# Layer 1 of a two-layer transformer: six edits to who does what, and a new order of the plan

## The chip, the cores and the metric

One core of a Trainium2 chip runs the whole program in one launch. The metric is the device time of one execution in microseconds; lower is better. The engines are TensorE (PE, matrix products; PEld is its weight loads), VectorE (DVE), ScalarE (ACT), GpSimd (POOL) and SyncE (SP, which here only issues DMAs). Each engine works through its own queue strictly in order and waits on semaphores of the others.

## The reference

4096 tokens (2 sequences of 2048) of width 256 pass two layers in float32. Each layer normalizes the tokens and adds to them an attention result and a feed-forward result:

```python
xn = _layernorm(x, axis=-1)
x = x + _L0_attn_ref(xn, ...) + _L0_ffn_ref(xn, ...)
xn = _layernorm(x, axis=-1)
x = x + _L1_attn_ref(xn, ...) + _L1_ffn_ref(xn, ...)
```

Layer 0 is causal attention with 16 heads and a mixture of eight experts (two per token). The change touches layer 1 only. Its attention is against 32 fixed key patterns instead of other tokens: 16 heads give each token 16 rows of 32 scores, and each row passes a sparsemax:

```python
z_sorted = -jnp.sort(-z, axis=-1)
cum = jnp.cumsum(z_sorted, axis=-1)
k = jnp.arange(1, S + 1, dtype=z.dtype)
support = 1.0 + k * z_sorted > cum
k_sup = jnp.sum(support, axis=-1, keepdims=True)
tau = (take_along_axis(cum, k_sup - 1) - 1.0) / k_sup
return jnp.maximum(z - tau, 0.0)
```

The weighted values are projected with `Wo` and get the output bias `bo`. The feed-forward part has a shared expert for all tokens and eight routed ones of which each token takes its best two.

## The kernel before, in words

Layer 0 (lines 274 to 1305) ends with the experts' results written to `oe`, a table in device memory with two result rows per token (the two experts'). Layer 1 begins at line 1311.

**Set-up (1315 to 1383).** SP loads the shared expert's weights (`fg_sb`, `fu_sb`, `fd_sb`). Weights of the attention are folded: `WK` gives all scores from a token in one product, `vbd` holds the values. `three` splits a float32 bias into three bfloat16 parts, so that one extra bfloat16 product (with `row3`, three rows of ones) adds it inside PSUM: `bqK` for the scores, `bo3` for the output. The scratch of this set-up lies in `xn`.

**A plan (class `Plan`, 49 to 127).** The rest of layer 1 is a list of tasks. `add` gives each its engine (`V`, `A`, `G`, `PE`, `S`), an estimated duration in ns, the tasks it comes after, and the buffers (`hold` on a `ring` of n) that it takes (`new`) or uses (`use`). `write` then emits the tasks one after the other as a small simulation: it finds the task that can start first, looks at the others of the same engine that could start almost as early, and of these takes the one with the lowest rank (`RANKS`, 1389) and then the longest way to the end (`way`). So a lower rank goes first. Product durations are stretched by 1.8 for the first 60 us of the plan. The order that comes out is pinned: it is each engine's program order.

The tasks:

- `prepare(grp)`, eight groups of 512 tokens: `add_results` (1425) loads the two rows per token of `oe`, the first into `xn`, the second into one of four landing buffers inside the `z` buffers, and VectorE adds each to `x_sb` (the residual, on chip): two additions of 128x1024. Then the mean and variance (`stat`), reciprocal roots by Newton steps on tiny 128x4 tiles (`roots`, 13 VectorE instructions), normalizing on ScalarE (`norm`), turning on TensorE (`flip`, `keep_`) into `xT`, and router logits.
- `shared(blk)`: the shared expert, its result added to `x_sb` by VectorE.
- `router()`: after the logits of all groups, the best two experts of each token, counts, slots and gates, on VectorE with a few products.
- `dispatch`: 64 indirect DMAs from GpSimd's queue send rows of `xn` to their slot in `buf1`.
- `routed(j)`, 20 blocks of 512 rows: GpSimd fetches the weights (two indirect DMAs), SP loads the rows, VectorE casts the rows' target numbers to integers (`places`, 1712), TensorE turns and multiplies, ScalarE and VectorE activate, and four indirect DMAs of GpSimd's queue send the result to `oe`.
- `scores` and `sparsemax` (1775, 1793), eight of them, each for 512 tokens (128 x 64 rows of 32 scores, 2048 numbers in each partition). The rows are sorted by a 15-stage network: in each stage VectorE makes two comparisons (max and min) and ScalarE copies what stays. Stages alternate between two buffers (`srt`). Then a running sum (`threshold`), minus one times 1/k (`divide`, one VectorE instruction with `invk`), the largest of it (`largest`), and GpSimd subtracts it (`less`). One ring `r_lane` serializes the sparsemaxes on the two buffers. `z` has three buffers.
- `attend(b, c)`: turns, relu, weighting; the second sequence's wait until the first's `project` is through, since both use `oT`. `project(b, h)`: two float32 products and one bfloat16 product (the bias) into PSUM, and VectorE adds the result to `x_sb`.
- `combine(grp)`: `add_results` again for layer 1's routed results; `store(blk)` writes the output.

Most instructions of the plan are recorded by the one helper at line 138, so the profile names them all L138; they are told apart by their tiles.

## Time and profile before

| what | us |
|---|---|
| three runs | 2168.5, 2185.76, 2180.45 (median 2180.45) |
| profiled execution, its own time | 2170.47 |
| its span, first to last instruction | 2168.7 |
| busy: PE, DVE, ACT, POOL | 1927.2, 1408.9, 912.6, 696.2 |
| mean granted TensorE clock | 0.94 |
| set-up of layer 1 begins | 1603 |
| first group normalized (ScalarE) | 1629.8 |
| last group's roots end (VectorE) | 1677.3 |
| first row sent (GpSimd) | 1706.7 |
| first sort comparison (VectorE) | 1717.0 |
| last maximum of a sparsemax ends (VectorE) | 2119.0 |

Times inside the execution count from its first instruction. "Busy" of an engine is time with an instruction running, waits not counted; where an engine stood idle, the profile names in brackets what ended the wait. The eight maxima of the sparsemaxes (`tau`) start at 1765.6, 1822.1, 1867.5, 1912.5, 1957.2, 2003.0, 2058.7 and 2116.8.

### The profile page before, as it was taken

What the parts mean: (1) busy time and instruction counts of PE and PEld (TensorE: products, weight loads), DVE (VectorE), ACT (ScalarE), POOL (GpSimd) and SP (SyncE); (2) the same over time, 40 slices, a digit from 0 to 9 for tenths busy, and PEclk for the clock granted to TensorE, in tenths of its full rate; (3) what the DMA queues carried; (4) which work ended last, traced back from release to release, by engine and by line L of the source; (5) the groups of instructions that cost most, each with busy time, mean ns of one, the idle gap of its engine ahead of it and who ended that gap; (6) DMA issues with size and microseconds to landing.
All of it is one profiled execution on the core that took longest, in us unless ns stands there. A gap on an engine that the chain in (4) does not pass through costs nothing. (4 is left out here: it accounts for less than half of the span.)

```text
span 2168.7 us, 26456 instructions
## 1 busy us (share of the span) xinstructions
PE 1927.2 (89%) x9497; PEld 1074.1 (50%) x9510; DVE 1408.9 (65%) x2010; ACT 912.6 (42%) x1815; POOL 696.2 (32%) x920
## 2 busy tenths in 40 slices
PE   4689998999999999999998899999977985788886
PEld 2344443444444444444443566666746653566664
DVE  4476788677775678777771222222248797999875
ACT  3044455355566555655667111111114232554442
POOL 4232212343335234231001111111210486365652
PEclk8599899899999999999999899999995998999999
DMA  5433311442324333141100712221032123334427
GB/s 155 126 99 101 109 60 38 123 121 96 94 63 138 102 106 99 58 120 53 37 11 11 249 42 85 91 92 49 25 116 70 44 83 112 92 115 123 128 101 232
DMA packets 151064, 204.45 MB, mean 94 GB/s; under 512 B 16393, under 2 KB 116881, under 8 KB 150930
## 3 DMA queue, kind: packets, MB, share of 16 engines
q1 hardware_dynamic: 131264, 151.55, 23.1%
q0 software_dynamic: 16640, 49.41, 6.6%
q10 hardware_dynamic: 3026, 1.77, 0.3%
q8 instruction: 76, 1.25, 0.2%
q14 instruction: 58, 0.48, 0.1%
HBM read 109.13 MB, written 98.79 MB: 96 GB/s over the span
## 5 line engine op out<-in xcount | busy, mean ns | idle before, releaser
L509 ACT ACTIVATE es<-sc 128x512 f32<-128x512 f32 (+3 forms) x1280 | 599.5, 535 | 457.6 <-PE sc L309 443.7
L470 DVE TENSOR_REDUCE part<-s 128x2 f32<-128x1024 f32 (+3 forms) x640 | 650.1, 1058 | 207.2 <-PE s L309 206.1
L309 PE MATMUL sc<-q,ks 128*128 128x512 f32 (+3 forms) x1280 | 426.4, 419 | 19.9 <-ACT es L509 19.5
L309 PEld LDWEIGHTS sc<-q,ks 128*128 128x128 f32 x1280 | 212.5, 192 | 248.3 <-ACT es L509 173.7
L309 PE MATMUL av<-es,va 128*32 128x512 f32 (+3 forms) x2560 | 300.9, 548 | 3.7 <-POOL es L511 2.1
L309 PE MATMUL s<-ks,q 64*128 64x512 f32 (+3 forms) x1280 | 253.0, 447 | 32.8 <-DVE part L470 10.9
L511 POOL TENSOR_SCALAR_AFFINE_SELECT es<-es 128x256 f32<-128x256 f32 x256 | 103.3, 407 | 555.8 <-ACT es L509 554.8
L138 DVE TENSOR_TENSOR srt<-srt 128x1024 f32<-128x1024 f32 (+3 forms) x224 | 231.7, 1072 | 7.0 <-ACT srt L138 0.2
L309 PEld LDWEIGHTS s<-ks,q 64*128 64x128 f32 x1280 | 111.7, 189 | 199.3 <-DVE part L470 113.3
L1276 POOL DMA_INDIRECT oe<-ys,to x72 | 70.0, 972 | 335.1 <-DVE ys L1275 330.2
L1268 DVE TENSOR_TENSOR hT<-ge,pg 128x384 f32<-128x384 f32 x96 | 53.1, 554 | 185.9 <-PE pg L1265 184.7
L1267 ACT ACTIVATE ge<-pa 128x384 f32<-128x384 f32 x96 | 47.1, 490 | 269.2 <-PE pa L1265 269.1
L138 POOL DMA_INDIRECT oe<-xn,to x80 | 100.3, 1254 | 101.4 <-ACT xn L138 82.8
L138 POOL DMA_INDIRECT buf<-xn,slot x64 | 86.1, 1345 | 118.1 <-DVE rc L138 98.9
L1265 PE MATMUL pa<-inT,wi 128*128 128x384 f32 x336 | 123.3, 486 | 0.0
L1265 PE MATMUL pg<-inT,wi 128*128 128x384 f32 x336 | 122.1, 486 | 0.0
L138 ACT COPY srt<-srt 128x1024 f32<-128x1024 f32 (+2 forms) x80 | 66.7, 834 | 120.9 <-DVE srt L138 120.1
L1272 PE MATMUL py<-wt,hT 128*128 128x256 f32 x504 | 112.2, 379 | 0.0
L309 PEld LDWEIGHTS av<-es,va 128*32 128x32 f32 x2560 | 55.6, 109 | 99.7 <-issue 75.9
L1272 PEld LDWEIGHTS py<-wt,hT 128*128 128x128 f32 x504 | 95.8, 190 | 17.5
L1275 DVE TENSOR_SCALAR ys<-py,gates 128x256 f32<-128x256 f32 x72 | 34.8, 484 | 86.2 <-PE py L1272 86.2
L1265 PEld LDWEIGHTS pg<-inT,wi 128*128 128x128 f32 x336 | 63.3, 190 | 42.7
(262 smaller groups left out, 2349.4 us busy)
## 6 DMA issues: line engine op xcount, KB each, us to landing
q<-qd SPq DMA_DIRECT2D x64, 256.0 KB
xn<-oe SPq DMA_DIRECT2D x24, 512.0 KB
buf<-zero SPq DMA_DIRECT2D x20, 516.0 KB
buf<-zero SPq DMA_DIRECT2D x20, 514.0 KB
xn<-buf SPq DMA_DIRECT2D x20, 514.0 KB
rows<-buf SPq DMA_DIRECT2D x8, 1161.0 KB
qd<-hi SPq DMA_DIRECT2D x16, 512.0 KB
qd<-lo SPq DMA_DIRECT2D x16, 512.0 KB
```

The source lines that it names most:

```text
L138: return lambda *a, **k: self.tc.keep_in_program_order(f(*a, **k))
L309: pin(PE.matmul(*args, **kw))
L470: pin(V.tensor_reduce(parts[j][:, i, 2 * pair:2 * pair + 2, kb], sc[:, :, :n], AX.X, ALU.max))
L509: pin(A.activation(es[:, g % 2, :n], sc[:, :n], AF.Exp, scale=0.25))
L511: pin(G.affine_select(es[:, :, 0:P], es[:, :, 0:P], pattern=[[0, 2], [1, P]], compare_op=ALU.is_ge, fill=0.0, base=0, channel_multiplier=-1))
L1265: PE.matmul(ps[:, :n], lhsT=wi[:, dc, col:col + P], rhs=inT[:, dc], start=dc == 0, stop=dc == 1)
L1267: A.activation(ge[:, :n], pa[:, :n], AF.Gelu)
L1268: V.tensor_tensor(hT[:, f, :n], ge[:, :n], pg[:, :n], ALU.mult)
L1272: PE.matmul(py, lhsT=hT[:, f, P * i:P * i + P], rhs=wt[:, f], start=f == 0, stop=f == 3)
L1275: V.tensor_scalar(ys, py, gates_e[:, c:c + 1], None, ALU.mult)
L1276: G.indirect_dma_start(out_ways[c % 4], bass.IndirectOffsetOnAxis(ap=to[:, c:c + 1], axis=0), ys, None, bounds_check=2 * NT - 1, oob_is_er ...
```

## The change

It is all in layer 1.

- **Result pairs on GpSimd.** `add_results` loads both rows of a group, GpSimd adds them to each other (`both`), and VectorE adds the sum to `x_sb` once (`take`). This holds for `prepare` and for `combine`.
- **Loads by token group.** A new second key `sub` orders tasks of equal rank: the two loads of group 0, then those of group 1, and so on; the shared expert's weights come after the third load.
- **Roots in batches.** `prepare` is split into `measure` and `prepare`; the root steps run for groups 0, 1, 2-3, 4-5 and 6-7.
- **Output bias on GpSimd.** `bo3` and its third product in `project` go; after a group is normalized, GpSimd adds `bo` to its `x_sb` (`bias_out`), and the additions of shared and projected results wait for that.
- **Casts on ScalarE.** `places` is an `A` task.
- **Factor 1/k on GpSimd.** The subtraction of one moves into the last sort stage's copy; the multiplication is a GpSimd task, except in the first two sparsemaxes. Two lanes replace one, so that the next sparsemax's first stage may use the buffer that the running sum has read.
- **Unread products first.** Twelve products whose result nobody reads open the plan on TensorE.
- **New order.** New ranks, and 1.15 in place of 1.8 for the first products.

The core of the diff:

```diff
-    def add(self, eng, ns, f, after=(), new=(), use=(), lag=0, rank=0):
+    def add(self, eng, ns, f, after=(), new=(), use=(), lag=0, rank=0, sub=0):
...
-            s, t = max((z for z in cand if ...), key=lambda z: (-z[1].rank, z[1].way))
+            s, t = max((z for z in cand if ...), key=lambda z: (-z[1].rank, -z[1].sub, z[1].way))
...
-    SP.dma_start(fg_sb, fg[:, :, NE:NE + 2])
-    SP.dma_start(fu_sb, fu[:, :, NE:NE + 2])
-    SP.dma_start(fd_sb, fd[:, NE:NE + 2])
...
+        WARM = 12
...
-        three(bo3, bo_sb, bias[:, 0:E])
...
         RANKS = {
-            "add_results.take": 8, "attend.flip": 3, "attend.keep_": -1, "attend.weigh": 3, "prepare.flip": -4,
-            "prepare.keep_": -3, "prepare.logits": -2, "routed.down": 1, "routed.fetch": 3, "routed.flip": -1,
-            "routed.hidden": 1, "routed.keep_": 2, "routed.out_": 2, "routed.places": 4, "router.slots": 4,
-            "router.totals": -2, "scores.go": 3, "scores.keep_": -2, "shared.<lambda>": -2, "shared.down": 3,
-            "sparsemax.<lambda>": 4, "sparsemax.copy": -1, "sparsemax.divide": 4, "sparsemax.largest": 6,
-            "sparsemax.less": 3, "sparsemax.threshold": 5
+            "activate.silu": 3, "add_results.load": 2, "add_results.take": 3, "attend.flip": 28, "attend.keep_": 3,
+            "attend.weigh": 10, "moe_transformer_kernel.<lambda>": 2, "moe_transformer_kernel.shared_weights": 2,
+            "prepare.flip": -3, "prepare.logits": -3, "prepare.norm": 5, "routed.fetch": 2, "routed.hidden": 14,
+            "routed.out_": 3, "routed.places": 5, "routed.send": -6, "router.means": 2, "router.stretches": 5,
+            "router.totals": 6, "router.weights": 2, "scores.go": 6, "sparsemax.<lambda>": 4, "sparsemax.copy": 3,
+            "sparsemax.threshold": 1, "store.go": 6
         }
...
-        r_lane = plan.ring(1)
+        r_lanes = plan.ring(1), plan.ring(1)
...
-                def take(st=st):
-                    pV.tensor_tensor(xs, xs, st["at"], ALU.add)
-                d = add("S", 1700, load, after, new=[] if direct else [hold], lag=3500)
-                last = [add("V", 1220, take, [d] + last, use=[] if direct else [hold])]
-            return last
+                loads.append(add("S", 1700, load, after, ..., lag=3500, sub=2 * grp + k))
+
+            def both():
+                pG.tensor_tensor(st[0], st[0], st[1], ALU.add)
+
+            def take():
+                pV.tensor_tensor(xs, xs, st[0], ALU.add)
+            g = add("G", 2000, both, loads, use=holds)
+            return [add("V", 1220, take, [g], use=holds)]
...
+            def bias_out():
+                pG.tensor_tensor(x_sb[:, 4 * grp:4 * grp + 4], x_sb[:, 4 * grp:4 * grp + 4], bc(bo_sb, 1, [P, 4, E]), ALU.add)
+            ready[grp] = [add("G", 2000, bias_out, n4)]
...
+        def warm():
+            hold, st, last = plan.hold(r_pz), {}, []
+
+            def product():
+                if not st:
+                    st["pz"] = psum("pz")
+                pPE.matmul(st["pz"], lhsT=ident, rhs=wo_sb.rearrange("p c e -> p (c e)"), start=True, stop=True)
+            for i in range(WARM):
+                last = [add("PE", 860, product, last, new=[] if i else [hold], use=[hold] if i else [])]
...
-                pV.tensor_copy(st["to"], st["rows"][:, :, E])
+                pA.copy(st["to"], st["rows"][:, :, E])
...
-            i4 = add("V", 160, places, [r], new=[hto], use=[hr])
+            i4 = add("A", 300, places, [r], new=[hto], use=[hr])
...
-                        pA.copy(ne, ce)
+                        if last:
+                            pA.activation(ne[:, :, 0], ce[:, :, 0], AF.Copy, bias=-1.0)
+                            pA.copy(ne[:, :, 1], ce[:, :, 1])
+                        else:
+                            pA.copy(ne, ce)
...
-                pV.scalar_tensor_tensor(level(15), level(15), -1.0, bc(invk, 1, [P, n, NPAT]), ALU.add, ALU.mult)
+                (pV if early else pG).tensor_tensor(level(15), level(15), bc(invk, 1, [P, n, NPAT]), ALU.mult)
...
-            t = add("V", n * 36, divide, [t], use=[lane])
-            t = add("V", n * 36, largest, [t], use=[lane])
+            t = add("V", n * 36, divide, [t], use=lanes[1:]) if early else add("G", 3900, divide, [t], use=lanes[1:])
+            t = add("V", n * 36, largest, [t], use=lanes[1:])
...
-                pPE.matmul(po, lhsT=row3, rhs=bo3, start=False, stop=True)
...
-        for grp in range(NG):
-            prepare(grp)
+        warm()
+        for g0, g1 in ((0, 1), (1, 2), (2, 4), (4, 6), (6, 8)):
+            for grp in range(g0, g1):
+                measure(grp)
+                if grp == 0:
+                    weights.append(add("S", 2000, shared_weights, lag=3000, sub=2.5))
+            r = add("V", 2000, lambda f=roots, a=g0, b=g1: f(a, b), stats[4 * g0:4 * g1])
+            for grp in range(g0, g1):
+                rooted[grp] = r
+                prepare(grp)
...
-        plan.write(60000, 1.8)
+        plan.write(60000, 1.15)
```

## The prediction

> **What bounds the kernel now.** I read the page's forty slices first: matrix work fills slices 0 to 29, and everything the change touches is layer 1, from 1604 us to the end. Then busy time by stage for that part, the chain of waits, and each engine's timeline. From busy time by stage, columns us, PE, PEld, DVE, ACT, POOL busy (x instructions), granted clock, DMA:
>
> ```profile
> 1630.00:1635.00 5.00, 4.27 (x16) 3.08 (x16) 4.49 (x19) 3.02 (x6) 0.00 (x0) 0.50 1.03 350
> 1665.00:1670.00 5.00, 5.00 (x24) 4.62 (x23) 4.56 (x17) 2.66 (x6) 0.00 (x0) 0.50 0.00 0
> 1680.00:1685.00 5.00, 5.00 (x37) 4.28 (x37) 0.38 (x2) 2.86 (x4) 0.00 (x0) 1.00 0.00 0
> 1717.00:1822.00 105.00, 78.90 (x233) 46.67 (x233) 90.02 (x95) 27.94 (x41) 86.55 (x62) 0.92 0.27 95
> 1822.00:2119.00 297.00, 243.66 (x1105) 186.83 (x1114) 270.60 (x271) 140.56 (x227) 167.53 (x117) 0.93 0.35 109
> 2119.00:2168.70 49.70, 30.99 (x162) 20.77 (x160) 25.03 (x33) 8.92 (x17) 7.55 (x5) 0.94 0.78 254
> ```
>
> The reader is to see four stages. To 1677, VectorE prepares the groups (4.5 of every 5 us busy), GpSimd does nothing, TensorE runs at half clock. From 1707 to 1812 GpSimd sends rows back to back and VectorE sorts beside it. To 2119 VectorE is busy 271 of 297 us: it sets the pace. The last 50 us are TensorE's projection. Each stage has its own witness in the timelines, VectorE's first:
>
> ```profile
> 1655.97 0.17 DVE L138 TENSOR_SCALAR sm<-mv 128x4 f32<-128x4 f32 x1
> ...
> 1658.43 1.22 DVE L138 TENSOR_TENSOR x_sb<-x_sb,z 128x1024 f32<-128x1024 f32 x1
> ...
> 1819.39 0.17 DVE L138 CAST to<-xn 128x4 int32<-128x4 f32 x1 [8.28 <-DMA xn<-buf]
> 1822.02 0.17 DVE L138 CAST to<-xn 128x4 int32<-128x4 f32 x1 [2.46 <-DMA xn<-buf]
> ...
> 2067.19 0.69 DVE L138 TENSOR_TENSOR h<-si,gu 128x512 f32<-128x512 f32 x1 [6.14 <-PE gu L138]
> ...
> 2077.10 2.37 DVE L138 TENSOR_TENSOR srt<-z 128x1024 f32<-128x1024 f32 x2 [5.42 <-ACT z L138]
> ```
>
> One run of the root steps lasts 1655.97 to 1658.43, 2.46 us. Casts hold VectorE 10.7 us for rows; late scores and products hold it 11.6 us around 2061 to 2077. GpSimd's timeline, its row for layer 0's bias, and the sort tile between 1869 and 1878 (ns min/median/max):
>
> ```profile
> 1706.68 0.97 POOL L138 DMA_INDIRECT buf<-xn,slot  x1 [98.88 <-DVE rc L138]
> ...
> 1869.25 0.99 POOL L138 DMA_INDIRECT oe<-xn,to  x1 [21.30 <-ACT xn L138]
> ...
> 1871.79 3.90 POOL L138 TENSOR_TENSOR z<-z,tau 128x2048 f32<-128x2048 f32 x1
> ```
> ```profile
> L547 POOL TENSOR_TENSOR xo<-xo,bout_sb 128x1024 f32<-128x1024 f32 x8 | 18.9, 2372 | 0.3 <-DMA xo<-in_x_dram 0.2
> ```
> ```profile
> L138 DVE TENSOR_TENSOR srt<-srt x4: 1097/1180/4664, 1871.0 to 1877.8; 128x1024 f32<-128x1024 f32 x2, 128x512 f32<-128x512 f32 x2
> ```
>
> This is the line I weigh most. A compare that lasts 1.22 us alone lasted 4.66 while GpSimd's subtraction ran: VectorE stood still until GpSimd was through. The same happened at 1825 (4.54), 1917 (3.41), 1961 (2.62), and to casts at 2005 (3.31) and 2067 (3.89): 17 us of the 24 us that these six subtractions lasted. A product with one input in PSUM, at 1961.13, took its usual 0.69. So work moved to GpSimd is not beside VectorE's work; much of it is in front of it.
>
> **The change part by part.** The sum is made against the profiled execution: span 2168.7, 1.8 around it, 2170.5 in all. The three runs have a median of 2180.45, 10 above; I keep to the profiled scale and take 1% of the median (22 us), about what a measurement here can tell from no change, for the chances.
>
> Preparation. Per group VectorE now does two additions (1.2 each), statistics (2.2) and roots (2.46); eight groups are 56.5 us. It will do one addition and the statistics per group and roots five times: 8 x 3.4 + 5 x 2.46 = 39.5. The output bias's three-part split (2.8 us, up to 1625) goes too, so it can start when the score bias's split ends, 1616.9: data is there, since the old queue order landed 4.2 MB by 1623 at some 350 GB/s and a pair is now first in line, 1 MB, some 3 us from 1607. Of SP's issues, three weight loads (0.6 us each) move behind three result loads; the shared products wait for them, by 1618, before any group is turned. The later wait on SP (5.8 us for the split's scratch) goes; a fifth pair now waits for GpSimd's first sum, some 2.4 us after landing. Unheld, the last roots end at 1616.9 + 39.5 + 1 (small additions and copies) = 1657.4, against 1677.2. But GpSimd gets 16 operations of 2.37, some 11 of them (six sums, five biases) inside this time, 26 us. Held share: 17 of 24 us in the rows, times the part of VectorE's time here that has two SBUF inputs, 22 of 39.5: 0.40, 26 x 0.40, some 11 us. Roots end at 1668.4: minus 9. Ends: minus 20 (nothing held) and plus 6 (all 26 held). The biases stand before VectorE's additions of shared and projected results; those come after 1690, when the first are long done.
>
> The skill's GPSIMD Engine Reference (Key points) speaks against the change as the rows do: GpSimd shares its SBUF interfaces with VectorE, in conflict with instructions of two SBUF inputs or in a two-port mode. It does not name one-input statistics, and no row here shows them against GpSimd; by the rule they run free, and my 11 us would stand; if they are held as well, it would be 19.
>
> Unread products and clock. Twelve products at about 0.86 (a score tile's two products end 1.72 apart at full clock: 1701.09 to 1702.81) run from 1612.5 to 1623 in TensorE's gap of 18 us, ahead of the first turn, now some 1625: free. What they can give is clock: the rows show 0.50 up to 1678, logits 3.58 us there and 1.85 after. Only what VectorE waits for counts: between 1677 and the first send at 1706.7 it idles 12 us on products, partly at full clock already. I take minus 2; ends minus 6, and plus 5 (two late biases of 2.37 in front of the routing).
> The skill's TensorE: Matmul & The Clock Gate (Part 1) lets about 3.4 us of sustained work restore the clock; here TensorE was busy 5.0 of 5 us at 1665 and still at 0.50 until 1678. By the page the term would be near 0; the rows decide.
>
> Dispatch: 64 sends, 1.65 us apart with their issue, as before; it moves with its start. GpSimd's remaining biases may cost 0 to 5 there, taken 0.
>
> Casts. Twenty casts leave VectorE (0.16 each, 3 us) for ScalarE, where the nearest row is a 128-element copy, 0.43: 8.6 us in 140 busy of 297, hidden unless a sort copy queues behind one. The two rows waits move with them: ScalarE's sort copies stand behind a cast that waits for rows, and VectorE runs at most a stage (2.4 us) ahead. I take minus 3 for the casts (ends minus 10 and plus 6) and minus 4 of the 10.7 us (ends minus 10.7 and 0).
>
> Factor 1/k. Six of eight leave VectorE: minus 6 x 2.28 = 13.7. GpSimd's takes 3.65, like its subtraction over the same 2048 elements, and the maximum waits for it. The second buffer lane lets both halves of the next first stage run ahead, but the half that follows GpSimd's start is held, 3.4 each: plus 20.6. Behind it on GpSimd stand sends and weight fetches; their idle time covers 6 x 3.65 = 22. Net plus 7; ends minus 14 (only unheld products meet it) and plus 67 (rival three).
>
> Order. VectorE idles 297 - 271 = 26 us to 2119. The largest piece, 2061 to 2077, is the last scores waiting for buffers of the second half's turns, which wait for the first half's projection (1979 to 2051, between routed products). New ranks (lower goes first) leave projection at 0 and move routed hidden products from 1 to 14, behind weighing (10) and scores (6); turns fall to 28. The first helps, the last hurts. I take minus 12; ends minus 26 (no idle) and plus 26 (twice).
>
> Tail. A projection step repeats every 1.75 us, 0.25 of it the bias product: 16 x 0.25 = minus 4. Eight pair sums (2.37) may hold eight additions, in front of projection's own: plus 1 taken; loads space pairs some 3 us apart, so GpSimd is mostly through. Minus 3; ends minus 6 and plus 10.
>
> Sum: -9 -2 -3 -4 +7 -12 -3 = -26: 2144.5, say 2144.
>
> **The rivals.** One: VectorE is hardly held. For it: statistics and PSUM products may fall under GpSimd's work. Preparation -20, clock -4, casts and rows -11, factor -10, order -20, tail -4: -69, 2101. Against: six held rows of eight.
> Two: no gain. Order saves nothing and preparation is held twice as much: -26 + 12 + 11 + 4 (rows wait moves whole) = +1: 2171. For it: the stage from 1707 to 1812 is GpSimd's, and the rows wait moves engines, not away.
> Three, slower: the factor waits in GpSimd's queue behind a send that waits for ScalarE. Before, 18 such waits total 82.8 us, 4.6 on average, up to 21.3; VectorE cannot pass the maximum's wait for long. If each of six meets 10 us, between those two, that is +60: 2204. It turns the sign from 26 / 6 = 4.4 us per factor. Against: the plan orders sends and factors by expected readiness, and the queue's other waits were under 10.
>
> **How the numbers follow.** Forecast 0.44, own range 2122 to 2158. Rival one 0.26, 2075 to 2122. Two 0.17, 2158 to 2192. Three 0.13, above. The range 2090 to 2195 leaves out about 0.08 below and 0.11 above. Faster by over 1% means below 2158.6: the first two, 0.70. Slower means above 2202: 0.11. Same 0.19.
>
> **What would show it.** Preparation: one addition per group, five root runs, the last ending near 1668; statistics at 0.39 beside GpSimd's sums, and additions over 2 us where held. Clock 1.0 from 1612 on. First send near 1696. Casts gone from VectorE, with its wait near 1800 now on sort copies. Six GpSimd operations of about 3.65 with a compare over 4 us beside each. Idle in the sort stage near 14. Projection steps 1.5 us apart. I am wrong if compares keep 1.22 beside GpSimd (then rival one), if VectorE waits long for the factor (three), or if scores come later than before (two).

## The result, and the profile after

The changed kernel takes 2189.40 us (median of 20 runs, 2180.2 to 2199.17) where the kernel before takes 2177.57 beside it (2168.5 to 2185.76): ratio 1.0057, 95% interval 1.0042 to 1.0071. It is 12 us slower, clear of the noise, and I had forecast 26 us less. The profiled execution of the changed kernel took 2194.07, 5 above its median; that of the kernel before took 2170.47, 7 below its own. So the two traces differ by 23.4 us of span, and about half of that is scatter between executions. One execution of e10's kernel, 2975.28 us at a granted clock of 0.55, is left out of the numbers below.

Where it went, by four points that every trace shows (the set-up's first product; the end of the last root steps; the first sort compare; the end of the last maximum):

| stretch, us | before | after |
|---|---|---|
| start to set-up's first product | 1605.1 | 1608.0 |
| to the end of the last roots | 72.2 | 71.9 |
| to the first compare | 39.7 | 46.8 |
| to the end of the last maximum ("the sort stretch") | 402.0 | 402.5 |
| to the end ("the tail") | 49.7 | 62.9 |

Layer 0 is the same code in both; its 2.9 us are scatter. The changed kernel lost 7 us between roots and sort, 13 in the tail, and won nothing in the sort stretch. A part of the 7 is scatter too. The eight products of the set-up, before and after:

```profile
1605.10 3.70 PE L1365 MATMUL big<-xn 128*128 128x512 f32 x8
```
```profile
1608.00 5.40 PE L1362 MATMUL big<-xn 128*128 128x512 f32 x8
```

From 1605 to 1615 the clock was 1.00 in the first trace and 0.86 and 0.80 (stretches of 5 us) in the second. Both cases are met with either code. Where these products take 3.70, the first compare comes 111.9 us after the first of them with the preparation of before (also in e12) and 115.8 with that of the changed kernel (e13); where they take 5.40, 115.8 (e15) and 118.7. So with like set beside like the change costs 3 to 4 us up to the first compare, not 7: the roots end 1 to 2 us earlier, and 5 are lost behind them.

Busy time by stage of the changed kernel, columns as shown before (us, PE, PEld, DVE, ACT, POOL busy, clock, DMA):

```profile
1665.00:1670.00 5.00, 5.00 (x29) 3.82 (x28) 4.59 (x14) 1.68 (x4) 1.84 (x1) 0.83 0.00 0
1680.00:1685.00 5.00, 4.62 (x23) 4.56 (x24) 0.27 (x2) 4.03 (x8) 2.86 (x2) 0.50 0.02 3
1717.00:1822.00 105.00, 86.98 (x257) 51.24 (x255) 98.35 (x115) 28.71 (x44) 84.88 (x66) 0.96 0.23 81
1822.00:2129.00 307.00, 246.23 (x1132) 190.05 (x1132) 268.03 (x248) 148.84 (x261) 205.84 (x130) 0.93 0.37 113
2129.00:2192.00 63.00, 41.83 (x120) 27.06 (x120) 19.44 (x25) 5.71 (x10) 26.13 (x12) 0.60 0.61 200
```

The reader is to see the clock: at 1680, where the kernel before had 1.00, it is 0.50, and in the tail 0.60 for 0.94. In the row from 1822, which is 10 us longer than its row of before, GpSimd has 38 us more work and VectorE only 2.6 less. VectorE's timeline of the changed kernel, against the rows of before:

```profile
1621.22 2.01 DVE L1338 CAST xn<-xn 128x512 bf16<-128x512 f32 x1
...
1623.55 2.26 DVE L1342 SCALAR_TENSOR_TENSOR bqK<-xn,ident,bqK 128x512 bf16<-128x512 bf16 x1
...
1635.42 1.18 DVE L138 TENSOR_SCALAR sms<-mvs 128x4 f32<-128x4 f32 x1
1636.63 4.23 DVE L138 TENSOR_SCALAR sms<-sms 128x4 int32<-128x4 int32 x2
...
1839.58 0.69 DVE L138 TENSOR_TENSOR h<-si,gu 128x512 f32<-128x512 f32 x1 [6.81 <-PE gu L138]
...
1881.13 2.29 DVE L138 TENSOR_REDUCE tau<-srt 128x64 f32<-128x2048 f32 x1 [7.97 <-POOL srt L138]
...
2023.95 6.67 DVE L138 TENSOR_TENSOR srt<-z 128x1024 f32<-128x1024 f32 x2
```

The set-up's split of the score bias is held too: a cast takes 2.01 (0.42 at 1618.84, before GpSimd's first sum) and the step that adds its part 2.26 (0.74 at 1619.57). Root steps of four numbers per partition, 0.17 us each alone, take 4.23 for two; the wait for rows (8.28 and 2.46 before) is gone and a wait for products of 6.81 stands near it; the maximum waits 7.97 for GpSimd's factor; two compares take 6.67 where 2.4 is usual. GpSimd's timeline beside them:

```profile
1620.03 5.23 POOL L138 TENSOR_TENSOR xn<-xn,z 128x1024 f32<-128x1024 f32 x2 [2.77 <-DMA z<-oe]
...
1636.53 4.30 POOL L138 TENSOR_TENSOR xn<-xn,z 128x1024 f32<-128x1024 f32 x2
...
1875.55 0.98 POOL L138 DMA_INDIRECT oe<-xn,to  x1 [0.30 <-issue]
1876.54 4.56 POOL L138 TENSOR_TENSOR srt<-srt,cst_sb 128x2048 f32<-128x2048 f32 x1
...
2122.34 4.55 POOL L138 TENSOR_TENSOR srt<-srt,cst_sb 128x2048 f32<-128x2048 f32 x1
...
2130.92 0.97 POOL L138 DMA_INDIRECT oe<-xn,to  x1 [0.30 <-issue]
2131.91 3.65 POOL L138 TENSOR_TENSOR z<-z,tau 128x2048 f32<-128x2048 f32 x1
```

The two held root steps begin and end with GpSimd's sums (1636.53 to 1640.83); the held split stands beside the sums from 1620.03 to 1625.26. The factor at 1876.54 started 3.4 us after the running sum ended (1873.16), behind sends. In the last step the factor lasts 4.55, the maximum follows, and then the subtraction waits behind four sends until 2131.91. TensorE's timeline shows what that did to the tail, two lines of before, then the changed kernel, then a line of VectorE's:

```profile
2122.88 0.66 PE L138 MATMUL tp<-ident,z 128*128 128x128 f32 x4 [1.53 <-POOL z L138]
...
2130.49 1.13 PE L138 MATMUL po<-wo_sb,oT 128*128 128x256 f32 x4 [0.51 <-DVE x_sb L138]
```
```profile
2129.47 1.09 PE L138 MATMUL po<-aT,vbd 128*64 128x128 f32 x8 [0.67 <-issue]
2135.61 1.97 PE L138 MATMUL tp<-ident,z 128*128 128x128 f32 x8 [5.05 <-POOL z L138]
...
2145.55 1.13 PE L138 MATMUL po<-wo_sb,oT 128*128 128x256 f32 x4 [0.51 <-DVE x_sb L138]
...
2148.61 1.97 PE L138 MATMUL po<-aT,vbd 128*64 128x128 f32 x8 [1.94 <-DVE x_sb L138]
2151.92 2.07 PE L138 MATMUL po<-wo_sb,oT 128*128 128x256 f32 x4 [1.34 <-ACT oT L138]
2154.51 2.07 PE L138 MATMUL po<-wo_sb,oT 128*128 128x256 f32 x4 [0.51 <-DVE x_sb L138]
```
```profile
2145.41 2.82 DVE L138 TENSOR_TENSOR x_sb<-x_sb,xn 128x1024 f32<-128x1024 f32 x1
```

After 5.05 us without work eight turns take 1.97, nearly twice as long; at 2142 a projection's products take 1.13 again; then VectorE's addition is held beside a pair sum of GpSimd (2.82 for 1.22), TensorE idles 1.94 and 1.34, and the projections behind take 2.07, 12 of the 16. The projection's products keep TensorE busy for 29.7 us in this tail and 18.1 in the one before: 11.6 of the 13.2 that the tail lost. (Their durations sum to 39.2 and 25.9; the ends of neighbours overlap.)

### The profile page after: what moved, and what is told of

Its sections match the earlier page's. It is cut to its first block, busy times and chain, and to the rows that moved or that the text cites. A ratio compares the mean times of both kernels' runs of the same rounds, so it can differ in the third digit from the quotient of the medians.

```text
span 2192.1 us, 26391 instructions
## 1 busy us (share of the span) xinstructions
PE 1955.2 (89%) x9502; PEld 1089.5 (50%) x9502; DVE 1399.5 (64%) x1921; ACT 916.1 (42%) x1842; POOL 783.2 (36%) x950
## 5 line engine op out<-in xcount | busy, mean ns | idle before, releaser
L138 DVE TENSOR_TENSOR srt<-srt 128x1024 f32<-128x1024 f32 (+3 forms) x224 | 236.3, 1092 | 7.6 <-DVE srt L138 0.5
L138 POOL DMA_INDIRECT oe<-xn,to x80 | 102.8, 1285 | 57.0 <-ACT xn L138 33.4
L138 POOL DMA_INDIRECT buf<-xn,slot x64 | 83.2, 1300 | 49.7 <-issue 49.1
```

The lines of the kernel that those rows point to most:

```text
L138: return lambda *a, **k: self.tc.keep_in_program_order(f(*a, **k))
```

## Experiments

The theory at the start: GpSimd's new duties (pair sums, factor, bias) stand in VectorE's way and cost more than they free, and the tail runs at half clock. The rivals: the new order is what costs; the casts or the unread products do. Each expectation counts against the changed kernel or the kernel before as it says. The ratios below are against the kernel before, run beside each (its medians there: 2173 to 2178); the changed kernel's is 1.0057. A difference of two such ratios is good to some 5 us. "The last scan" in the expectations is the end of the last maximum. "VectorE is busy for 382 of 402 us" in two expectations is a sum of durations whose ends overlap; by stage VectorE is busy 360.6 of 402.0 there.

### One part undone, the planner told of it (e1 to e4)

```diff
-            early = 4 * b + c < 2
+            early = True
```


> Changed kernel, but the factor 1/k of all eight steps is done by VectorE (as for the first two). Theory (GpSimd's moved operations cost more than they free): the six waits of VectorE for the factor (19.1 us in all) and the compares held beside it (1975.04 4.95, 2023.95 6.67 x2, 2080.21 5.79 x2 against 1.22 to 3.65 alone) go, six times 2.28 = 13.7 us come back on VectorE: the stretch from the first compare to the end of the last scan shrinks from 304.5 us by 5 to 12, and since the last step's wait of 5.5 us and 4.6 us of factor stand before the tail too, the tail shrinks by some 5: time 8 to 17 us below the changed kernel, near the kernel before. Rival A (the new order is what costs, the factor is hidden): within 4 us of the changed kernel, stretch still near 304. Rival B (VectorE is the bound and the factor relieves it): 8 us or more above the changed kernel.

The 304.5 us of this expectation count from the third step's first compare (1824.62); from the first compare of all it is 402.5. Measured: 2186.37, ratio 1.0033 (1.0018 to 1.0049): 5 us below the changed kernel, give or take 5, and the stretch is 401.3. The waits for the factor went, and one of 17.7 us for scores (`z`) took their place: the planner had written another order. It decides nothing yet on the factor.

```diff
-                pG.tensor_tensor(st[0], st[0], st[1], ALU.add)
+                pV.tensor_tensor(st[0], st[0], st[1], ALU.add)
...
-            g = add("G", 2000, both, loads, use=holds)
+            g = add("V", 1220, both, loads, use=holds)
```


> Changed kernel, but the sums of the result pairs (16 with those at the end) are done by VectorE, 1.2 us each instead of 2.2 to 2.4 on GpSimd. Theory: the tiny steps of the roots, the casts and the copies that stood held (4.23 x2, 2.30 x2, 2.26, 1.89 for 0.17) run at 0.17 again, so 8 more additions on VectorE (9.8 us) cost nothing on balance in the preparation; last roots end between 1672 and 1682 (changed kernel 1679.9), and the set-up ends by 1618 instead of 1625.7: time from 8 us below to 2 above the changed kernel. Rival (the sums on GpSimd do free VectorE and the late end comes from the clock and from the loads): last roots end 6 to 10 us later, time 5 to 10 us above.

Measured: 2209.11, 1.0146 (1.0124 to 1.0168): 19 us above the changed kernel, which neither expected. The part ahead did better than expected: first compare 106.2 us after the set-up's first product (118.7 in the changed kernel). But the planner moved the choice of each block's expert (`stretches`) behind two sort steps, to 1810; weights came late, and the stretch is 427.8.

```diff
-            ready[grp] = [add("G", 2000, bias_out, n4)]
+            ready[grp] = n4
...
-                    pPE.matmul(po, lhsT=oT[:, cc, h], rhs=wo_sb[:, cc], start=cc == 0, stop=cc == 1)
+                    pPE.matmul(po, lhsT=oT[:, cc, h], rhs=wo_sb[:, cc], start=cc == 0, stop=False)
+                pPE.matmul(po, lhsT=row3, rhs=bo3, start=False, stop=True)
```


> Changed kernel, but the output bias is added by TensorE again, as the third product of a projection step (128x256), and GpSimd's eight bias additions are gone; the set-up splits the bias in three again (some 4 us on VectorE). Theory: TensorE is busy for more of each step of the tail, keeps its granted clock, and the tail (end of the last scan to the end of the span, 62.9 us in the changed kernel, 49.7 before) comes back to 50 to 55 us; time 6 to 12 us below the changed kernel. Rival A (the half clock of the tail comes from the 5 us for which TensorE waits for the last step's factor, maximum and subtraction, not from the missing product): tail stays at 60 or more, and the third product adds 0.2 to 0.5 us a step: time 0 to 8 us above. Rival B: GpSimd's bias additions were the worst hold in the preparation: last roots end 5 us or more before 1679.9, with the tail unchanged.

Measured: 2209.48, 1.0129 (1.0102 to 1.0156). First compare 112.4 after the set-up's first product, 6 us better; the stretch 422.3, with 33.4 us of waits for hidden products. The tail is 68.5, and the projection's products still sum to 38.2 (39.2): with the bias product back the clock halves too, after 21.94 us in which TensorE stood idle. My theory of the tail fell here.

```diff
         RANKS = {
-            "activate.silu": 3, "add_results.load": 2, "add_results.take": 3, "attend.flip": 28, "attend.keep_": 3,
...
+            "add_results.take": 8, "attend.flip": 3, "attend.keep_": -1, "attend.weigh": 3, "prepare.flip": -4,
...
-        plan.write(60000, 1.15)
+        plan.write(60000, 1.8)
```


> Changed kernel, but with the table of ranks and the planner's factor of the kernel before (1.8). Theory: the order is worth little by itself; the waits for the factor and the half clock of the tail stay: time within 8 us of the changed kernel, more likely above, since the old order's stall of 15 us at 2061 to 2077 comes back. Rival (the new order is what costs): time 10 us or more below the changed kernel, at or below the kernel before.

Measured: 2234.17, 1.0269 (1.0245 to 1.0292): 45 us worse, both expectations missed. First compare 129.8, tail 78.1. The old order is no use to the new tasks. These four also show what was wrong with them as experiments: the order is computed from what the planner is told, and any change of a task moves hundreds of others.

### The clock, the batches, the order, the casts (e5 to e8)

```diff
+                    if (b, c, g) == (1, 3, 0):
+                        pz = psum("pz")
+                        for _ in range(6):
+                            pPE.matmul(pz, lhsT=ident, rhs=wo_sb.rearrange("p c e -> p (c e)"), start=True, stop=True)
                     st["tp"] = psum("tp")
```


> Changed kernel, with six products whose result nobody reads (128x512, 0.86 us each) put on TensorE just ahead of the turns of the last sort step, where it stood idle for 5.05 us; nothing else moves. Theory (the tail runs at half the granted clock because TensorE stood idle for those 5 us; e3, whose bias product was back, kept the half clock, so the missing product is not the cause): the projection's products take 26 to 33 us in all instead of 39.2, the tail shrinks from 62.9 us by 5 to 13, time 5 to 13 us below the changed kernel. Rival (without the bias product TensorE has too little to do in each step, so the clock falls again at the next short gap, 1.94 and 1.34 us at 2146 to 2152): the clock is up only to about 2147, tail within 4 us of 62.9, time within 4 us.

Measured: 2186.96, 1.0067 (1.0043 to 1.009), no different from the changed kernel's 1.0057 in time; the tail of the profiled execution is 56.9 us for 62.9. TensorE's timeline of this run:

```profile
2130.49 5.42 PE L138 MATMUL pz<-wo_sb,ident 128*128 128x512 f32 x12
2135.74 1.04 PE L138 MATMUL tp<-ident,z 128*128 128x128 f32 x8
...
2151.37 1.13 PE L138 MATMUL po<-wo_sb,oT 128*128 128x256 f32 x4 [0.52 <-DVE x_sb L138]
2154.63 1.13 PE L138 MATMUL po<-wo_sb,oT 128*128 128x256 f32 x4 [2.13 <-DVE x_sb L138]
2156.27 1.94 PE L138 MATMUL po<-aT,vbd 128*64 128x128 f32 x8 [0.51 <-DVE x_sb L138]
2158.88 2.08 PE L138 MATMUL po<-wo_sb,oT 128*128 128x256 f32 x4 [0.67 <-ACT oT L138]
```

Both theories held in part. With the gap filled the turns take 1.04 and the clock stays whole to 2155; then one addition held on VectorE idles TensorE 2.13 us and the clock halves in this run too.

```diff
-        for g0, g1 in ((0, 1), (1, 2), (2, 4), (4, 6), (6, 8)):
+        for g0, g1 in ((0, 1), (1, 2), (2, 4), (4, 6), (6, 7), (7, 8)):
```


> Changed kernel, but the roots of the last two token groups are made one group at a time, as before; the others stay in pairs. Theory: with two groups behind the last roots, 8 normalizations, 4 sets of turns and 2 blocks of gate products follow them in place of half as many, and the sigmoid of the router starts 16.0 us after the last roots' end (10.0 in the kernel before); split, it starts 11 to 13 us after, and the first send and the first compare come 3 to 5 us earlier: time 2 to 5 us below the changed kernel. Rival (the half clock of TensorE alone makes the 16 us): still 15 or more, time within 2 us.

Measured: 2195.81, 1.0101 (1.0081 to 1.0121), some 10 us above the changed kernel: both expectations on the time missed. The sigmoid starts 13.1 us after the last roots (16.0), as expected, but those end 78.6 us after the set-up's first product instead of 71.9, and the first compare comes at 122.3 (118.7). The planner's order moved here too, so this decides nothing on the batches alone.

```diff
         RANKS = {
-            "add_results.take": 8, "attend.flip": 3, "attend.keep_": -1, "attend.weigh": 3, "prepare.flip": -4,
...
+            "activate.silu": 3, "add_results.load": 2, "add_results.take": 3, "attend.flip": 28, "attend.keep_": 3,
...
-        plan.write(60000, 1.8)
+        plan.write(60000, 1.15)
```


> Kernel before with only the new table of ranks and the planner's factor 1.15. In e4 the old order cost the changed kernel 45 us. Theory (each order is fitted to the kernel that it stands in; neither is better by itself): 5 to 40 us above the kernel before, with VectorE idle for longer in the sort stretch (19.8 us in the kernel before, 43.7 in e4). Rival (the new order is better whatever the kernel, and is what holds the changed kernel up): 5 us or more below the kernel before.

Measured: 2197.52, 1.0096 (1.0073 to 1.0119), 23 us above the kernel before. The expected idle time of VectorE did not come; the loss is the tail, 77.9 us, into which the new order put 28 instructions of the routed hidden products. With e4: neither order is better by itself.

```diff
-                pV.tensor_copy(st["to"], st["rows"][:, :, E])
+                pA.copy(st["to"], st["rows"][:, :, E])
...
-            i4 = add("V", 160, places, [r], new=[hto], use=[hr])
+            i4 = add("A", 300, places, [r], new=[hto], use=[hr])
```


> Kernel before with only the 20 casts of the row numbers moved from VectorE to ScalarE. Theory (VectorE is busy for 382 of the 402 us from the first compare to the end of the last scan, so what is taken from it shows, unless something else holds it): the 20 casts take 10.3 us there; the stretch shrinks by 5 to 10, time 5 to 10 us below the kernel before, about 2168 to 2173. Rival A (the casts stood in idle time): within 3 us. Rival B (the planner, told of 300 ns on ScalarE for 160 on VectorE, writes a worse order): 3 us or more above, with VectorE idle for longer than 19.8 us.

Measured: 2195.49, 1.0098 (1.0079 to 1.0116): rival B. Stretch 410.1, tail 60.7; again the order, not the casts.

### The same parts with the order kept (e9 to e13)

From here on the planner is told what the changed kernel (e12: the kernel before) tells it, and only the engine that executes differs. All other instructions keep their place in each engine's order.

```diff
-                pG.tensor_tensor(st[0], st[0], st[1], ALU.add)
+                (pG if which_ else pV).tensor_tensor(st[0], st[0], st[1], ALU.add)
```


> Changed kernel; the eight pair sums of the preparation are executed by VectorE, but the planner is still told of 2000 ns on GpSimd, so every other instruction keeps its place (in e2 the planner was told of VectorE, and wrote another order, whose third sort step waited). Theory (the sums on GpSimd hold VectorE's small steps and so delay the preparation): the first sort compare comes 6 to 13 us earlier against the start of the span (1726.7 in the changed kernel, 1713.6 in e2), the stretch from there to the end of the last scan stays at 400 to 405 us, time 6 to 13 us below the changed kernel. Rival A (the gain of e2's preparation was its order's, not the engine's): first compare within 3 us of 1726.7, time within 3 us. Rival B (what is won ahead is lost again behind, since something else than VectorE's work sets the end of the stretch): first compare earlier, stretch longer by as much.

Measured: 2184.26, 1.0036 (1.0018 to 1.0054): 5 us below the changed kernel, give or take 5. First compare 109.9 after the set-up's first product, 8.8 earlier (the set-up's products take 5.40 in both), though VectorE does 8 more additions (10.7 us); the stretch is 405.8, 3.3 longer. So the result lies between the theory and rival B. The root steps' one-input operations, changed kernel first, then e9 (ns min/median/max):

```profile
L138 DVE TENSOR_SCALAR sms<-sms x10: 170/172/2100, 1629.6 to 1677.7; 128x8 int32<-128x8 int32 x6, 128x4 int32<-128x4 int32 x4
L138 DVE TENSOR_SCALAR sms<-mvs x5: 164/1178/2257, 1629.4 to 1677.3; 128x8 f32<-128x8 f32 x3, 128x4 f32<-128x4 f32 x2
```
```profile
L138 DVE TENSOR_SCALAR sms<-sms x10: 170/171/173, 1630.5 to 1675.6; 128x8 int32<-128x8 int32 x6, 128x4 int32<-128x4 int32 x4
L138 DVE TENSOR_SCALAR sms<-mvs x5: 165/170/173, 1630.3 to 1675.2; 128x8 f32<-128x8 f32 x3, 128x4 f32<-128x4 f32 x2
```

The maxima fall from 2.1 and 2.3 us to 0.17. The 2.1 and the pair at 1636.63 stood until a sum on GpSimd was through; the 2.26 and the 1.18 stood until a bias addition was (1664.62 to 1666.85, 1635.42 to 1636.57), and in e9, where the biases are still on GpSimd, none of them met a root step. The sums on GpSimd are a loss up to the first compare; in the time it is not clear of the scatter.

```diff
-            def bias_out():
...
-            ready[grp] = [add("G", 2000, bias_out, n4)]
+            ready[grp] = [add("G", 2000, lambda: None, n4)]
...
+                pPE.matmul(po, lhsT=row3, rhs=bo3, start=False, stop=True)
```


> Changed kernel with the bias product back on TensorE (and its split in the set-up, some 4 us of VectorE), GpSimd's eight bias additions left out, and the planner still told of what the changed kernel does, so the order is kept (e3 wrote another). Theory: the preparation ends earlier by the hold of the bias additions less the set-up's 4 us, first compare 2 to 7 us before 1726.7; in the tail the third product at the half clock adds 0.37 us to each of 16 steps, 6 us, unless it keeps the clock up: time from 7 us below to 4 above. Rival (TensorE with the third product keeps its clock after a warm stretch as in the kernel before): tail 50 to 55 us, time 8 us or more below.

Measured: 2184.09, 1.0044 (1.0022 to 1.0066): 3 us below the changed kernel, give or take 6, not told apart. First compare 112.1 for 118.7; tail 55.0: the clock falls there too, at a gap, and is whole again by 2158.

```diff
+                (pG if which_ else pV).tensor_tensor(st[0], st[0], st[1], ALU.add)
...
+            ready[grp] = [add("G", 2000, lambda: None, n4)]
...
+                pPE.matmul(po, lhsT=row3, rhs=bo3, start=False, stop=True)
...
+                pV.tensor_tensor(level(15), level(15), bc(invk, 1, [P, n, NPAT]), ALU.mult)
```


> Changed kernel with its order kept, and all three of GpSimd's new duties undone: the preparation's sums and the factor of all eight steps executed by VectorE, the bias by TensorE. What is left of the change: casts on ScalarE, roots in batches, loads by token group, unread products, the new order. Theory: first compare 8 to 15 us before 1726.7; the stretch from there to the last scan's end within 5 us of 402.5, as VectorE takes back 13.7 us and loses some 14 of hold (e1); tail 55 to 69: time 5 to 15 us below the changed kernel, about the kernel before. Rival (the hold is not what costs; the order, made for GpSimd's help, stalls without it): stretch 410 or more, time at or above the changed kernel.

Measured: 2180.75, 1.0011 (0.9992 to 1.0031), 10 us below the changed kernel, give or take 5, and the same as the kernel before. First compare 112.5, stretch 397.2, tail 57.8. So GpSimd's three duties together are the loss, and what is left of the change (casts, batches, loads, unread products, order) is worth nothing that shows: ratio 1.0011.

```diff
-                pV.tensor_copy(st["to"], st["rows"][:, :, E])
+                pA.copy(st["to"], st["rows"][:, :, E])
```


> Kernel before with only its 20 casts executed by ScalarE and the planner still told of 160 ns on VectorE, so that all else keeps its place (e8 wrote another order, and left 21 more of the weighings for the tail). Theory: VectorE is busy for 382 of 402 us between the first compare and the last scan's end, so its 10.3 us of casts come off: stretch 392 to 397, time 5 to 10 us below the kernel before. Rival (what VectorE gives back is held up again: its compares stand longer beside GpSimd's work, as in e8, where srt from srt took 245.4 us for 240.2): stretch 399 or more, time within 3 us.

Measured: 2172.04, 0.9988 (0.997 to 1.0005); stretch 396.3 for 402.0. VectorE's longest waits in the stretch, kernel before and then e12 (us in total, times, longest):

```profile
DVE to L138 <- DMA xn<-buf: 10.7, 2, 8.3
DVE h L138 <- PE gu L138: 8.3, 3, 6.1
DVE srt L138 <- ACT z L138: 7.3, 2, 5.4
```
```profile
DVE srt L138 <- ACT z L138: 11.1, 2, 9.2
DVE h L138 <- PE gu L138: 8.3, 3, 6.3
DVE h L138 <- PE acc L138: 5.6, 1, 5.6
DVE srt L138 <- ACT srt L138: 5.0, 2, 4.5
```

The wait for rows, 10.7 us, turned into waits for scores, copies and products; VectorE's idle time stays at 41.2 (41.4). Only the casts' own time is won.

```diff
-                (pV if early else pG).tensor_tensor(level(15), level(15), bc(invk, 1, [P, n, NPAT]), ALU.mult)
+                pV.tensor_tensor(level(15), level(15), bc(invk, 1, [P, n, NPAT]), ALU.mult)
```


> Changed kernel; the factor of all eight steps executed by VectorE, the planner still told of 3900 ns on GpSimd, so the order is kept. e1, in an order of its own, left the stretch at 401.2 us (402.5): 13.7 us of work came back to VectorE, and the compares beside GpSimd's factor gave back 14.2. Theory (an exchange at par): stretch within 4 us of 402.5, VectorE's idle time in it less than 23.9 by about the waits for the factor, its compares from z and srt shorter by 10 to 15 in all; time within 4 us of the changed kernel. Rival A (the factor on GpSimd is a net loss, which e1's other order hid): stretch 396 or less, time 5 us or more below. Rival B (a net gain): stretch 407 or more.

Measured: 2178.56, 1.002 (0.9999 to 1.0041): 8 us below the changed kernel by the ratios, give or take 5: rival A. The stretch of the changed kernel, then of e13 (us, VectorE's busy time, clock, DMA):

```profile
1726.70:2129.20 402.50, 359.39 (x347) 0.93 0.33 106
```
```profile
1722.30:2117.20 394.90, 365.84 (x353) 0.92 0.33 108
```

VectorE takes back six multiplications, 13.7 us, and is busy only 6.5 longer: the other 7 had been hold. Its idle time falls from 43.1 to 29.1, and that is the larger part. In the changed kernel's waits the factor is first:

```profile
DVE tau L138 <- POOL srt L138: 19.1, 4, 8.0
DVE h L138 <- PE gu L138: 12.6, 3, 6.8
```

The other traces in this order agree: with the factor on GpSimd the stretch is 402.5 (changed kernel), 405.8 (e9) and 404.3 us (e10), with it on VectorE 394.9 (e13), 397.2 (e11) and 397.3 (e14). In four of six steps VectorE had too little else to do while GpSimd multiplied (waits of 8.0, 0.9, 4.7, 5.5); in the other two it began the next step's compares, and those were held (4.95 and 5.54 for 1.22).

### What is left, and a faster kernel (e14 to e18)

```diff
             def product():
+                if st:
+                    return
```


> The kernel of e11 (order of the changed kernel, GpSimd's three new duties undone) with eleven of the twelve unread products left out; the order is kept. Theory: they end 1.5 to 5 us before the first turns, so TensorE's clock is at half again by then, and they cost and gain nothing: first compare and time within 3 us of e11. Rival A (they warm TensorE for the first groups): first compare 3 us or more later. Rival B (they stand in the set-up's way, whose products they precede): first compare 3 us or more earlier.

Measured: 2176.06, 0.9986 (0.9964 to 1.0009). First compare 109.1 for e11's 112.5, rival B by the number; but the set-up's products took 3.70 here and 5.40 in e11, and e17 and e18 below, both at 3.70, are alike (109.0 and 108.9). From the first turns on its code is e11's; its profiled tail is 62.6 for 57.8, so a tail that loses its clock scatters by some 5 us.

```diff
+            which_ = "pz" if b == 1 and h % 2 else "po"
-            st, hold = {}, plan.hold(r_po)
+            st, hold = {}, plan.hold(r_pz if which_ == "pz" else r_po)
...
-                po = st["po"] = psum("po")[:, 0:E]
+                po = st["po"] = psum(which_)[:, 0:E]
```


> Kernel before with its casts executed by ScalarE in the old places (e12) and the second sequence's projection turn about between two banks of PSUM (po and pz, free by then) instead of one. In the kernel before each step of the tail's projection takes 1.75 us, 1.24 of products and 0.51 of waiting for VectorE to read the one bank. Theory: the wait goes, 16 times 0.51 = 8 us less what VectorE's additions then hold up: tail 42 to 47 us for 49.7, time 3 to 8 us below e12, 7 to 12 below the kernel before. Rival (the tail's end is set by VectorE's additions and the stores, not by TensorE): tail 48 or more, time within 2 us of e12.

Measured: 2168.51, 0.997 (0.9947 to 0.9993). Tail 49.0, for 51.1 in e12: the rival. TensorE is done at 2151.5 and the span ends at 2166.7; loads and stores, the DMA engines without a hole from 2130, set the end.

```diff
+                    if (b, c, g) == (1, 3, 0):
...
+            which_ = "pz" if b == 1 and h % 2 else "po"
```


> The kernel of e11 with the two banks of e15 and with e5's six unread products ahead of the last sort step's turns. Theory (the tail's loss is TensorE's clock, which falls when it idles for 4 to 5 us and again at the held additions): the clock stays at 1.00 through most of the tail, the projection's products take 26 to 29 us in all (30.1 in e11, 25.9 before), and the waits of 0.51 go: tail 43 to 49 us for 57.8, time 8 to 14 us below e11, under the kernel before. Rival (additions held on VectorE by GpSimd's sums set the pace): tail 53 or more, time within 4 us of e11.

To e11 come e5's products and e15's banks. Measured: 2167.86, 0.9968 (0.9949 to 0.9988): faster than both kernels, and 9 us below e11, give or take 6. The projection's products sum to 24.9 us (30.1 in e11), and the tail is 52.4, between theory and rival.

```diff
             g = add("G", 2000, both, loads, use=holds)
...
+            if which_:
+                last = []
+                for k in range(2):
+                    def one(k=k):
+                        pV.tensor_tensor(xs, xs, st[k], ALU.add)
+                    last = [add("V", 1220, one, [loads[k]] + last, use=[holds[k]])]
+                return last
```


> The kernel of e16 with GpSimd's last new duty undone: at the end each pair of result rows is added to x_sb by VectorE, one after the other, and not summed on GpSimd first. In e16 TensorE was done at 2149.3, yet the span ended at 2165.2: GpSimd's sums free the landing buffers late, and the DMA engines, busy from 2119.6, had holes at 2135 to 2140 and 2145 to 2150 (shares 0.49 and 0.55), where e15, which adds directly, was at 1.09 without a hole. Theory (the tail's end is then set by 12.6 MB at some 349 GB/s, 36 us from the first load): tail 46 to 49 us for 52.5, time 3 to 7 us below e16. Rival (VectorE's 8 more additions hold up the two banks, and TensorE falls to half its clock again): tail 52 or more, time at or above e16.

Measured: 2160.9 (2149.29 to 2167.59), 0.9925 (0.9899 to 0.9951): 16 us below the kernel before. The tails of e11, e16 and e17 by stage (us, VectorE busy, TensorE's clock, DMA share, GB/s):

```profile
2111.10:2168.90 57.80, 19.42 (x24) 0.82 0.67 218
```
```profile
2112.80:2165.20 52.40, 19.26 (x24) 0.88 0.74 241
```
```profile
2112.00:2158.20 46.20, 24.35 (x32) 0.94 0.84 273
```

The reader is to see the last two columns: with the clock and the banks mended, what remained was GpSimd's sums, which freed the landing buffers late. VectorE's eight more additions cost nothing there.

```diff
             def product():
+                if st:
+                    return
```


> The kernel of e17 with eleven of the twelve unread products at the start left out, order kept; beside e17 on the same chip. e14 against e11 (different calls) left open whether they cost 2 to 3 us or nothing. Theory: they end before the first turns and do nothing that lasts: within 3 us of e17. Rival: 3 us or more below e17 (they cost) or above (they help).

Measured: 2159.47, 0.9925 (0.9895 to 0.9954), the same as e17 run beside it, and the first compare comes at 108.9 for 109.0. The unread products do nothing.

## Why the prediction was wrong, by its own steps

The measured time, 2189.40, lies where I had put rival two, to which I gave 0.17. The three new duties of GpSimd undone together (e11) give back 10 us, give or take 5, and what is left of the change is worth about nothing where I had forecast 26 us of gain.

| step | predicted | measured | by |
|---|---|---|---|
| preparation, to the first compare | -9 | +6.8; +3 to +4 at the same clock in the set-up | traces, with e13 and e15; from the changed kernel -8.8 with the sums on VectorE (e9), -6.6 with the bias on TensorE (e10) |
| unread products, clock | -2 | 0 | e17 against e18 |
| casts and rows wait | -3 and -4 | -5.7 in the stretch; -2.6 (-6.5 to +1.1) in time | e12 |
| factor 1/k | +7 | +7.6 in the stretch, 8 in time | e13 |
| order | -12 | +0.9 in the stretch | e11 (397.2) against e12 (396.3) |
| tail | -3 | +13.2; 6 to 13 over other traces | traces; the same tail in e9 57.6 and e13 60.2, that of before in e12 51.1 |

**Preparation: mis-sized.** I let the hold act on operations with two SBUF inputs, by their share of VectorE's time: 0.40 of GpSimd's, 11 us. Each held operation less its time alone, the hold comes to some 16 us up to the last roots in the changed kernel. None of the eight additions in my share was held (1.20 to 1.42); one-input operations stood too, and tiny ones worst, to the end of GpSimd's operation whatever their own length. My own rows had shown it: casts of 0.17 at 3.31 and 3.89. I also put every sum behind the set-up, and 4.3 of the 16 us fell into the set-up: it ended 17.7 us after its first product where I had 11.8, 1.7 of that its clock. And 14 of GpSimd's operations came before the last roots' end, where I had 11. The rule I cited from the Trainium skill (GPSIMD Engine Reference, Key points) names a second class, instructions in a two-port mode, and its VectorE: DVE Perf Modes (What auto-detection actually checks) puts a single source and a destination in SBUF into such a mode, if their outermost dimensions are both even or equal. The 2.1 and 2.3 us for 0.17 agree with that, and the statistics, 0.39 to 0.43 beside GpSimd, ran free as I took them. Behind the roots 5 us went at the same clock in the set-up (44.4 in e13 for 39.7, 46.8 for 41.9 in e15), 7 between the two traces; the clock averaged 0.78 from the last roots to the first compare (0.99 before). With all three duties undone (e11) that part is still 46.2 with the clock at 0.79, so the duties are not the cause. The clock was back at 1.00 from 1670 to 1675 and fell behind a wait of 1.68 us; from 1677 to 1695 nothing but turns and products of 8 columns ran, at 0.50, and it came back with the products of 256 and 512 columns (0.92 from 1700). In the kernel before, products of 512 columns stand among those of 8 from 1676.5 on, and the clock is 1.00 from 1680. Whether that is what keeps the clock, no run tested; the cause stays open.

**Unread products and clock: right that they are free, wrong that they give 2.** They ended at 1627.5, the first turn came at 1632.7, and by then the clock was falling. That the clock could fall behind the roots, where the kernel before had it whole, was no case of mine.

**Casts and rows: the sum is right, the split is not.** The casts' time is won (the stretch is 395.5 in e15, which has them too); the wait for rows was no gain at all, because something else was late next.

**Factor: right in size and sign**, with the wrong make-up. I had minus 13.7 of work and plus 20.6 of hold; it was minus 13.7, plus 7 of hold and plus 14 of waiting. GpSimd's multiplication took 4.55 us, not the 3.65 of its subtraction, and rival three's wait in the queue was there, 0.2 to 5.9 us, but not the 10 that it needed.

**Order: this step failed.** "I take minus 12" rested on one stall of the old order that the new ranks should end. VectorE's idle time in the stretch did fall, by 9.4 us (31.8 in e11, 41.2 in e12), near the 12 that I took. But its busy time rose by 10.3 (365.4 for 355.1): the first compares from the scores took 25.2 us for 20.8, held beside GpSimd's subtraction, the compares of 512 columns 55.7 for 52.0, and 2.3 are the router's last steps, which the order put there. I priced the idle time and put the hold that comes with another order at nothing. In e4 and e7, each order with the other kernel's tasks, the kernels are 45 us slower than the changed kernel and 23 slower than the kernel before, so neither order is better by itself.

**Tail: this step failed.** "16 x 0.25 = minus 4" priced a product by its own duration. At full clock the step went from 1.75 to 1.65 (e5: 2142.14 to 2143.79), 0.10. And I looked for no loss of clock: it was 0.60 in the tail for 0.94, and that is most of the 13.2 us. TensorE stood idle because the last factor and the subtraction came late, and because the new order had left it less: 40 weighings after the last maximum, 59 before, so that a gap of 1.53 there became 5.05. With GpSimd's duties undone it was still 4.27 (e11), and the clock fell as well. The second fall came from the additions held beside the pair sums, for which I had taken 1 us. What brings the clock back is open: behind the second fall it came back in e10 and e11, with the bias product, and not in e14, with it, nor in the changed kernel, e1, e5, e9 and e13, without it.

Of the rivals, two came nearest: no gain from the order, more hold in the preparation. That rival stopped at 2171, because no case of mine held a lost clock. (Two small slips change nothing: one-input statistics held as well would make 18.4, not 19, and 26 / 6 is 4.3.)

## What to carry to other kernels

Here work moved to a free engine did not pay where the giving engine had nothing else to do until the result was back, or ran operations that were held meanwhile; look at both before moving work. Where a planner writes the order, try a part with the planner's inputs unchanged, or the trial measures the order. Ahead of a serial tail on TensorE look for a gap of some microseconds: here the clock lost there was paid on most of its steps, and work in the gap and a second PSUM bank, on top of the additions and the factor given back to VectorE and the bias to TensorE, turned a loss of 12 us into a gain of 16. When two traces are set side by side, look first for a difference of clock in code that is the same in both.

## What the runs showed of the hardware

- A VectorE operation of 4 or 8 numbers per partition, one input, takes 0.17 us and up to 2.3 while GpSimd adds 128x1024 (changed kernel against e9).
- GpSimd multiplies 128x2048 by a repeated factor in 4.55 us and subtracts a repeated column from as many in 3.65.
- The granted clock halves not only after 5.05 us without work: it fell behind gaps of 2.0 and 1.34 us around 1.1 us of products in e11, one of 2.13 between products in e5, one of 1.48 in e14; a gap of 1.53 ahead of the turns in the kernel before was followed by no fall.
- It can stay at half under load: in the changed kernel TensorE was busy for 19.25 of the 20 us from 1680 to 1700, all at 0.50, with turns and products of 8 columns to 1695. The Trainium skill (TensorE: Matmul & The Clock Gate, Part 1) lets some 3.4 us of sustained work restore it; after 2135 in the same kernel some 5 us did, from 1680 on 20 did not.
